# A graph attention kernel on one core: the split of the single-row loads between ScalarE's and SyncE's queues

## The chip, the core and the metric

The kernel runs on one core of a Trainium2 chip. The metric is the device time of one execution in microseconds (us); for a kernel the median over several executions is taken. The core's engines are TensorE (PE in the profile; its weight loads are PEld), VectorE (DVE), ScalarE (ACT), GpSimd (POOL) and SyncE (SP). SyncE computes nothing; it issues DMA transfers. ScalarE computes and issues transfers too: what it issues stands in the profile as ACTq, what SyncE issues as SPq, and an engine handles both kinds of work in the order of its program.

## The reference

One message passing layer over 6250 nodes with 128 features and 206250 edges, sorted by receiver, followed by a residual sum and a layer norm. Cut to what matters:

```python
w_ij  = silu(edge_attr_32 @ rad_W1 + rad_b1) @ rad_W2 + rad_b2
w_ij += silu(edge_attr_32_n2 @ sph_W1 + sph_b1) @ sph_W2 + sph_b2     # (E, 128), 8 heads of 16
alpha = ((x @ Wq)[dst] * w_ij * (x @ Wk)[src]).sum(per head) / 4 * edge_weight
out   = segment_sum(alpha * (x @ Wv)[src], dst) / 16
return layernorm(x + out)
```

The costly access is `[src]`: the senders are in no order, so the key and the value of each edge's sender are fetched from a table row by row.

## The kernel before

**Staging.** A first stage (the first 100 us or so) multiplies all nodes by Wk and Wv and stores one row of 256 floats a node, key and value side by side, in the table `kv_tab` in device memory. The main loop then goes over the edges. A *tile* is 128 edges, a *quad* four tiles (512 edges), a *group* four quads; there are 101 groups and 403 quads. The groups come in order, the quads of a group as 0, 2, 1, 3 (the list `order`). A last stage finishes the last three quads.

**One turn of the main loop** (one quad a turn, number `i`). TensorE sums the messages of the last group (L670), runs the first layers of quad `i+2` (L566), brings the queries to the edges of quad `i+1` (L585) and runs the second layers of `i+1` (L618). The last matmul of L585 gives the one signal of the turn, the *mark*. On it wait: ScalarE's first SiLU of quad `i+2` (L603), VectorE's product of queries and keys of quad `i+1` (L634), GpSimd's next gathers, and SyncE's loads of node rows `x` and edge features. After L634 VectorE goes on with L642, L644, L647 (the scores) and L659 (the messages).

**How the senders' rows arrive.** For most quads GpSimd gathers all four tiles with four indirect DMAs (L142), 14 turns ahead. In 58 quads, spread evenly over turns 8 to 401, the fourth tile is left out of the gathers (L182). Its 128 rows of 1 KB go into a buffer `wide`, each by a DMA of its own (L212) whose address is a number in a register. `ROW_ACT` of these 128 are issued by ScalarE, the rest by SyncE. The addresses are computed and turned in the first stage (`row_bytes`, `turn_rows`) into the table `at_i`, one line for each of the 58 tiles, SyncE's addresses from column `ROW_AT[SP]` and ScalarE's from column `ROW_AT[ACT]`. Register loads (L206) fetch them, up to 32 at a time for SyncE and up to 24 for ScalarE (`ROW_UNITS`).

**What sets the order around the rows.** At the end of each turn `load_rows` hands each engine its share of what is due: the work of a tile (one unit a row, six a register load) is spread evenly over the 6.8 turns (393 / 58) that lie between two such tiles, and it is dealt six turns early (`ROW_LEAD`). SyncE's share goes into its queue among its other transfers, one or two a turn: `x` (L315), `feats` (L252), `relb` (L263), `out` (L777). ScalarE's share stands after its SiLUs; up to two rows of it (`ROW_CARRY`) stand between the two SiLUs of a turn, around a small copy. VectorE waits for the count of all 128 rows (L631) ahead of L634 of that quad, and behind that wait stands all that VectorE does later.

The lines that the change touches are these numbers and the places that read them:

```python
 55 ROW_ACT = 68
 56 ROW_AT = {SP: 0, ACT: 64}
 57 ROW_LOAD = 6
 59 ROW_UNITS = {SP: 32, ACT: 24}
229         n = P - ROW_ACT
230         row_open.append({SP: rows_by(nc.sync, SP, 0, n), ACT: rows_by(nc.scalar, ACT, n, P)})
```

Of the kernel before, what the change touches and what calls it, by code (L numbers as in the profile page):

```python
# [21 lines left out]
SP = mybir.EngineType.SP  # L22
ACT = mybir.EngineType.Activation
# [28 lines left out]
ROW_FIRST = 8  # L52
ROW_LAST = 401
ROW_LEAD = 6
ROW_ACT = 68
ROW_AT = {SP: 0, ACT: 64}
ROW_LOAD = 6
ROW_CARRY = 2
ROW_UNITS = {SP: 32, ACT: 24}
# [14 lines left out]
def gnn_kernel(ctx, tc, x, src, dst, weight, edges, rad_W1, rad_b1, rad_W2, rad_b2,  # L74
# [120 lines left out]
    def open_tile(k):  # L195
# [5 lines left out]
        def rows_by(engine, name, a, b):  # L201
            regs = {}

            def load(e, m):
                c = ROW_AT[name] + e - a
                regs.update(zip(range(e, e + m), nc.values_load_multi_w_load_instructions(  # L206
                    at_i[k:k + 1, c:c + m], engines=(name,), min_val=0,
                    max_val=(N - 1) * ROW_BYTES,
                    skip_runtime_bounds_check_because="senders are nodes")[1]))

            def row(p):
                o = engine.dma_start(row_of[q][p:p + 1, 0, :].bitcast(U8),  # L212
                                     table[:, ds(regs.pop(p), ROW_BYTES)])
                tc.no_tile_sem_insts.add(o.ins.name)
                tc.add_to_no_dep_group(f"rows_{q}", o.ins)
                o.then_inc(row_sems[k % ROW_SEMS], 16)
                row_count[k % ROW_SEMS] += 16
                row_done[q] = row_sems[k % ROW_SEMS], row_count[k % ROW_SEMS]
                row_issued[q] = row_issued.get(q, 0) + 1

            items = []
            for e in range(a, b, ROW_UNITS[name]):
                m = min(ROW_UNITS[name], b - e)
                items.append((ROW_LOAD, lambda e=e, m=m: load(e, m)))
                items += [(1, lambda p=p: row(p)) for p in range(e, e + m)]
            rows_left[name] += items
            return sum(cost for cost, _ in items)

        n = P - ROW_ACT
        row_open.append({SP: rows_by(nc.sync, SP, 0, n), ACT: rows_by(nc.scalar, ACT, n, P)})  # L230
# [108 lines left out]
    with tc.tile_pool(name="nodes", bufs=1) as nodes, \  # L339
# [88 lines left out]
        def turn_rows():  # L428
            pt = nps.tile([P, QT, P], F32, name="pt", bufs=3)
            nc.tensor.transpose(pt[:ROW_TILES, 0, :], rows_f, ident)  # L430
            n = P - ROW_ACT
            for a, b, at in ((0, n, ROW_AT[SP]), (n, P, ROW_AT[ACT])):
                nc.vector.tensor_copy(at_i[:, at:at + b - a], pt[:ROW_TILES, 0, a:b])
# [693 lines left out]
```

## Time and profile before

| what | value |
|---|---|
| median of three runs | 2572.93 us (2570.8 to 2580.83) |
| the profiled execution, and its span | 2581.4 us, 2579.6 us |
| granted TensorE clock, mean | 0.844 of full speed |
| TensorE matmul busy | 2090.3 us, 81% |
| VectorE busy | 1527.9 us, 59% |
| GpSimd busy | 1474.3 us, 57% |
| ScalarE busy | 644.5 us, 25% |
| single-row DMAs issued by ScalarE | 3944 (58 tiles of 68) |
| single-row DMAs issued by SyncE | 3480 (58 tiles of 60) |
| indirect gathers on GpSimd | 1522 |

The page of the profile gives busy time, the chain of work that ended last, and groups of instructions by line. Issuing a DMA is not counted as busy, so ScalarE's 25% leaves out the time in which it issues rows, and SyncE has no busy time at all; how full these two are must be read from the timeline and from the counts of their instructions. A view can be limited to a stretch of the span, and two stretches of one loop can so be compared.

### The profile page before, as it was taken

To read this page: it belongs to the slowest core of one execution; us is meant where nothing else is said; L and a number is where in the kernel's file an instruction comes from. 1 tells how busy PE (TensorE), PEld (TensorE's weight loads), DVE (VectorE), ACT (ScalarE), POOL (GpSimd) and SP (SyncE) were. 2 spreads that over 40 slices of the span, in tenths; PEclk is the share of its full clock that TensorE was granted. 3 is DMA by queue.
4 is the path that set the end of the run, shared out by engine and by line. 5 is a ranking of instruction groups with operands and counts; after the bars stand their busy time and mean duration, and the time that the engine had idled before them with its cause. 6 is when DMAs were issued, how large, how long until landed. Compare 5 with 4: busy or idle time off the path is not lost.

```text
span 2579.6 us, 56198 instructions
## 1 busy us (share of the span) xinstructions
PE 2090.3 (81%) x16002; PEld 1743.4 (68%) x16002; DVE 1527.9 (59%) x3423; ACT 644.5 (25%) x1361; POOL 1474.3 (57%) x1562
## 2 busy tenths in 40 slices
PE   7687888888887878778788788888788888888788
PEld 6566766676666666667667676667566666666677
DVE  5465665656665655555556556556556555566568
ACT  2122222222222222222222222222222222222224
POOL 5565655656565556556566556556565555565550
PEclk8688888878888888888888888878888887888889
DMA  7433434344343434333343433334343443333331
GB/s 272 130 120 105 122 113 124 113 121 122 114 121 114 121 116 122 111 117 113 117 122 114 122 113 121 118 110 124 105 121 114 120 122 110 117 115 121 118 108 38
DMA packets 156799, 307.15 MB, mean 119 GB/s; under 512 B 41798, under 2 KB 90880, under 8 KB 156480
## 3 DMA queue, kind: packets, MB, share of 16 engines
q0 software_dynamic: 74080, 201.69, 27.0%
q1 hardware_dynamic: 72736, 97.22, 11.4%
q10 hardware_dynamic: 9664, 4.58, 0.7%
q8 instruction: 127, 2.08, 0.3%
q14 instruction: 192, 1.57, 0.2%
HBM read 289.88 MB, written 15.11 MB: 118 GB/s over the span
## 4 chain that ended last, share of the span: by engine, by line
PE 33%; issue 20%; DVE 15%; SPq 13%; another core or an unknown queue 12%; ACTq 5%; ACT 1%; DMA 1%; DVEq 0%
PE pw L618 14%; SPq L212 10%; PE pq L585 6%; PE ph L566 5%; ACTq L212 4%; DVE kq L634 3%; DVE side L644 3%; PE po L670 3%; DVE kq L642 3%; SPq L206 2%; PE pk L383 1%; ACTq L206 1%; PE pq L711 1%; DVE side L647 1%
## 5 line engine op out<-in xcount | busy, mean ns | idle before, releaser
L142 POOL DMA_INDIRECT kv<-kv_tab,src_i x1522 | 1442.9, 948 | 1017.6 <-remote 527.7
L618 PE MATMUL pw<-w,act 128*128 128x128 f32 x6448 | 1061.3, 323 | 131.5 <-issue 129.6
L618 PEld LDWEIGHTS pw<-w,act 128*128 128x128 f32 x6448 | 946.4, 229 | 214.3 <-issue 176.5
L603 ACT ACTIVATE act<-ph,b 128x512 f32<-128x512 f32 x806 | 554.6, 689 | 1856.5 <-remote 1559.2
L634 DVE TENSOR_TENSOR kq<-pq,kv 128x512 f32<-128x512 f32 (+1 forms) x404 | 271.1, 671 | 943.8 <-remote 765.7
L566 PE MATMUL ph<-feats,w 32*128 32x512 f32 x1612 | 673.5, 745 | 150.8 <-issue 143.1
L585 PE MATMUL pq<-q,hotT 32*128 32x128 f32 x3224 | 557.1, 321 | 10.0 <-DVE kq L634 6.8
L585 PEld LDWEIGHTS pq<-q,hotT 32*128 32x128 f32 x3224 | 470.8, 220 | 17.0 <-issue 16.7
L566 PEld LDWEIGHTS ph<-feats,w 32*128 32x128 f32 x1612 | 193.2, 209 | 317.4 <-issue 292.0
L644 DVE TENSOR_REDUCE side<-kq 128x32 f32<-128x512 f32 x404 | 280.2, 694 | 14.0
L659 DVE TENSOR_TENSOR msg<-kv,side 128x512 f32<-128x512 f32 (+1 forms) x404 | 269.0, 666 | 13.8
L642 DVE TENSOR_TENSOR kq<-pw,kq 128x512 f32<-128x512 f32 x404 | 274.5, 679 | 0.4 <-PE pw L618 0.4
L670 PE MATMUL po<-msg,hot 128*32 128x128 f32 x3200 | 183.2, 310 | 38.0 <-issue 37.7
L573 PE MATMUL pw<-brow,onesb 3*128 3x512 bf16 x403 | 176.6, 438 | 0.0
L670 PEld LDWEIGHTS po<-msg,hot 128*32 128x32 f32 x3200 | 86.5, 118 | 94.8 <-issue 67.4
L711 PE MATMUL pq<-part,to 128*128 128x128 f32 x196 | 58.4, 389 | 110.3 <-issue 76.1
L711 PEld LDWEIGHTS pq<-part,to 128*128 128x128 f32 x196 | 38.6, 246 | 126.4 <-issue 98.9
L647 DVE TENSOR_TENSOR side<-side,scale 128x32 f32<-128x32 f32 x400 | 79.8, 199 | 13.7
L292 DVE TENSOR_TENSOR hotT<-relb,side 128x512 f32<-128x512 bf16 x101 | 68.7, 680 | 0.0
L297 DVE TENSOR_TENSOR hot<-rel,side 128x512 f32<-128x512 f32 x100 | 68.0, 680 | 0.0
L286 PE MATMUL pq<-wq,xT 128*128 128x128 f32 x200 | 48.8, 331 | 10.0 <-DVE kq L634 7.7
L383 PE MATMUL pk<-wkv,xT 128*128 128x256 f32 x162 | 43.6, 412 | 13.1 <-DVE kv L385 10.0
(132 smaller groups left out, 851.6 us busy)
## 6 DMA issues: line engine op xcount, KB each, us to landing
wide<-kv_tab ACTq DMA_DIRECT2D x3944, 1.0 KB
wide<-kv_tab SPq DMA_DIRECT2D x3480, 1.0 KB
feats<-in_edges SPq DMA_DIRECT2D x101, 512.0 KB
kv<-kv_tab,src_i POOLq DMA_INDIRECT x1522, 2.8
relb<-rel_four SPq DMA_DIRECT2D x101, 128.0 KB
x<-in_x SPq DMA_DIRECT2D x101, 64.0 KB
out<-y SPq DMA_DIRECT2D x101, 64.0 KB
kv_tab<-kv SPq DMA_DIRECT2D x12, 512.0 KB
```

Of the source, the lines that this page charges most:

```text
L142: return nc.gpsimd.indirect_dma_start(out=o, out_offset=None, in_=table, in_offset=bass.IndirectOffsetOnAxis(ap=index, axis=0))
L212: o = engine.dma_start(row_of[q][p:p + 1, 0, :].bitcast(U8), table[:, ds(regs.pop(p), ROW_BYTES)])
L566: return nc.tensor.matmul(act_of[q, i], w1[r0:r0 + R, :], feats_of[g][r0:r0 + R, c0:c0 + EQ], start=True, stop=True)
L573: nc.tensor.matmul(pw, onesb[f:f + 3, :], brow[f:f + 3].rearrange("p t d -> p (t d)"), start=True, stop=False)
L585: o = nc.tensor.matmul(pq_of[q][:, t, :], hotT_of[g][b, t * P:(t + 1) * P], q_of[g][b, :], start=True, stop=True)
L603: o = nc.scalar.activation(act, act_of[q, i], AF.Silu, bias=b1[:, i:i + 1])
L618: o = nc.tensor.matmul(pw[:, t, :], act_of[q, i][:, t * P:(t + 1) * P], w2[:, i, :], start=False, stop=(t == QT - 1 and i == 1))
L634: o = nc.vector.tensor_tensor(kq_of[q][:, u, :], pq_of[q][:, u, :], kv[:, :, :D], op=OP.mult)
L642: nc.vector.tensor_tensor(m, pw_of[q][:, t, :], m, op=OP.mult)
L644: nc.vector.tensor_reduce(alpha, m.rearrange("p t (h e) -> p t h e", e=HD), AX.X, OP.add)
L659: nc.vector.tensor_tensor(msg_of[q][:, u, :].rearrange("p t (h e) -> p t h e", e=HD), kv[:, :, D:].rearrange("p t (h e) -> p t h e", e=HD) ...
L670: o = nc.tensor.matmul(po_of[g][j * W:(j + 1) * W, :], hot_of[g][:, j * QT + t, :], msg_of[g * NQ + j][:, t, :], start=(t == 0), stop=(t = ...
```

## The change

ScalarE issues 72 of the 128 rows of each of the 58 tiles, SyncE 56; before it was 68 and 60. ScalarE's part of the address table starts at column 56 where it started at column 64. The number of register loads stays: SyncE's 56 addresses come in two loads (32 and 24; before 32 and 28), ScalarE's 72 in three (24 each; before 24, 24 and 20).

```diff
-ROW_ACT = 68
-ROW_AT = {SP: 0, ACT: 64}
+ROW_ACT = 72
+ROW_AT = {SP: 0, ACT: 56}
```

On SyncE, in the middle of the main loop, from one load of node rows (`x`) to the next, four turns later. Rows written `wide<-kv_tab` are the single-row DMAs, with their number behind x; `at_i` is the register load of their addresses. Before:

```order
L315 DMA x<-in_x 128x512
L212 DMA wide<-kv_tab 1x1024 x9
L206 TENSOR_LOAD at_i
L777 DMA out<-y_14260 128x512
L212 DMA wide<-kv_tab 1x1024 x7
L263 DMA relb<-rel_four 128x1x512
L212 DMA wide<-kv_tab 1x1024 x10
L252 DMA feats<-in_edges 128x1024
L212 DMA wide<-kv_tab 1x1024 x11
L315 DMA x<-in_x 128x512
```

And now, at the same place:

```order
L315 DMA x<-in_x 128x512
L212 DMA wide<-kv_tab 1x1024 x10
L777 DMA out<-y_14261 128x512
L206 TENSOR_LOAD at_i
L212 DMA wide<-kv_tab 1x1024 x4
L263 DMA relb<-rel_four 128x1x512
L212 DMA wide<-kv_tab 1x1024 x10
L252 DMA feats<-in_edges 128x1024
L212 DMA wide<-kv_tab 1x1024 x10
L315 DMA x<-in_x 128x512
```

In these four turns SyncE has 37 single-row DMAs before and 34 now, and the register load stands behind the store of `out` where it stood ahead of it; the other transfers are the same.

On ScalarE, also in the middle of the main loop: two turns, from the second SiLU of one (`act_104`) to the first SiLU of the turn after the next (`act_99`); `tot` is a small copy. Before:

```order
L603 ACTIVATE act_104<-ph,b_73 128x512
L212 DMA wide<-kv_tab 1x1024 x10
L603 ACTIVATE act_105<-ph,b_73 128x512
L212 DMA wide<-kv_tab 1x1024
L715 ACTIVATE tot<-pq 128x128
L212 DMA wide<-kv_tab 1x1024
L603 ACTIVATE act_106<-ph,b_73 128x512
L212 DMA wide<-kv_tab 1x1024 x10
L603 ACTIVATE act_99<-ph,b_73 128x512
```

And now:

```order
L603 ACTIVATE act_104<-ph,b_73 128x512
L212 DMA wide<-kv_tab 1x1024 x12
L603 ACTIVATE act_105<-ph,b_73 128x512
L212 DMA wide<-kv_tab 1x1024
L715 ACTIVATE tot<-pq 128x128
L212 DMA wide<-kv_tab 1x1024
L603 ACTIVATE act_106<-ph,b_73 128x512
L212 DMA wide<-kv_tab 1x1024 x10
L206 TENSOR_LOAD at_i
L603 ACTIVATE act_99<-ph,b_73 128x512
```

With few exceptions up to 12 rows now stand between the second SiLU of a turn and the first SiLU of the next, where there were up to 11, and the register loads have moved along with the counts. TensorE, VectorE and GpSimd have the same instructions in the same order as before, apart from the widths of the two copies that fill `at_i` (56 and 72 columns).

## The prediction

> **What bounds the kernel now.** I began with the whole page: its first lines and its chain of waits (busy time with share and count; the chain's shares by engine).
>
> ```profile
> span 2579.6 us, 56198 instructions
> PE 2090.3 (81%) x16002; PEld 1743.4 (68%) x16002; DVE 1527.9 (59%) x3423; ACT 644.5 (25%) x1361; POOL 1474.3 (57%) x1562
> PE 33%; issue 20%; DVE 15%; SPq 13%; another core or an unknown queue 12%; ACTq 5%; ACT 1%; DMA 1%; DVEq 0%
> ```
>
> No engine is full, and SyncE, which computes nothing, holds 13% of the chain. So I asked what VectorE waited for (us in total, times, longest), first from 180 to 1014 us, then from 1014 to 2499 us; 1014 is where the first wait of a new kind falls.
>
> ```profile
> DVE kq L634 <- remote: 285.1, 114, 5.7
> DVE kq L634 <- PE pq L585: 26.3, 13, 5.6
> ```
>
> ```profile
> DVE kq L634 <- remote: 441.7, 175, 2.9
> DVE kq L634 <- DVEq L631: 66.4, 16, 9.7
> DVE kq L634 <- PE pq L585: 46.3, 27, 2.9
> DVE kq L634 <- DMA wide<-kv_tab: 20.4, 4, 7.1
> ```
>
> Up to 1014 us VectorE waits only for TensorE's mark. After it, 20 waits with 66.4 + 20.4 = 86.8 us end with the landing of single rows (L631 is the wait for their count). What that costs in pace, the groups by line show for the same two stretches (count, then busy and mean, then idle time before):
>
> ```profile
> L634 DVE TENSOR_TENSOR kq<-pq,kv 128x512 f32<-128x512 f32 (+1 forms) x136 | 91.4, 672 | 312.2 <-remote 285.1 <-PE pq L585 26.3
> L634 DVE TENSOR_TENSOR kq<-pq,kv 128x512 f32<-128x512 f32 (+1 forms) x237 | 159.3, 672 | 580.3 <-remote 441.7 <-DVEq L631 66.4 <-PE pq L585 46.3
> ```
>
> 136 quads in 834 us are 6.132 us each; 237 in 1485 us are 6.266. Which queue is late, the counts of L212's and L206's instructions tell (durations min/median/max in ns, first and last start): from 180 to 1014 us, then L206 in the same stretch, then from 1014 to 2499 us.
>
> ```profile
> L212 ACTq DMA_DIRECT2D wide<-kv_tab x1367: 3/228/772, 180.7 to 1013.9; - x196
> L212 SPq DMA_DIRECT2D wide<-kv_tab x1161: 2/203/1123, 180.3 to 1013.9; - x194
> ```
>
> ```profile
> L206 SPq TENSOR_LOAD <-at_i x39: 938/1917/2249, 193.5 to 1013.9; - x39
> ```
>
> ```profile
> L212 SPq DMA_DIRECT2D wide<-kv_tab x2101: 2/204/1462, 1015.4 to 2498.9; - x191
> ```
>
> The program deals SyncE 58 x 60 / 393 = 8.855 rows a turn. 136 turns ask for 1204; it issued 1161, so it fell back by 43, and 43/60 of a tile at 834 / (1161/60) = 43.1 us a tile is a head start of 31 us used up. Over the next 237 turns 2099 are asked for and 2101 issued: VectorE goes at SyncE's pace. ScalarE owes 58 x 68 / 393 = 10.04 a turn, 1365 for 136 turns, and issued 1367: it keeps up. That SyncE is full, and not held up, its own waits from 180 to 2499 us show; the first and last of the five that are listed:
>
> ```profile
> SPq L315 <- DVE y L732: 0.7, 1, 0.7
> ...
> SPq L252 <- remote: 0.2, 1, 0.2
> ```
>
> None is over 0.7 us. So there are two regimes: up to 1014 us the gathers and TensorE set 6.132 us a quad; after it SyncE's queue sets 6.266.
>
> **The change part by part.** It moves 4 rows a tile, 232 in all. *SyncE.* Its timeline in the middle of the loop (start, us, what, count):
>
> ```profile
> 1010.12 0.74 SPq L777 DMA_DIRECT2D out<-y  x1
> 1010.89 5.08 SPq L212 DMA_DIRECT2D wide<-kv_tab  x5
> 1016.02 0.56 SPq L263 DMA_DIRECT2D relb<-rel_four  x1
> 1016.68 6.17 SPq L212 DMA_DIRECT2D wide<-kv_tab  x11
> ```
>
> One of the other transfers takes 0.7 us to the next start, and there is one a turn. In the first stretch rows got 834 - 39 x 1.92 (loads) - 136 x 0.7 = 664 us, or 0.572 us a row; the eleven here agree (6.17 / 11 = 0.56). Four rows fewer save 2.29 us a tile: 43.1 becomes 40.8, against 6.776 turns x 6.132 = 41.55 that a tile lasts at the first regime's pace. SyncE then has 0.75 us a tile to spare and never loses its 31 us. The low bound for a row is 0.31 us, its price where no gathers run (rows below): then a tile takes 41.85 us and SyncE loses 0.3 us a tile, 17 us over 58 tiles, still within the 31. So the gain does not hang on this price. If the second regime goes, its 237 quads take 237 x 6.132 = 1453 us in place of 1485: **32 us less**. The other readings bracket it: idle time ahead of L634 rose from 312.2/136 = 2.30 to 580.3/237 = 2.45 us, 36 us over 237 quads; the waits themselves are 86.8 us, of which 20 x 2.30 = 46 would have been spent on the mark, leaving 41. I take 31.
>
> *ScalarE.* It gets 0.59 rows more a turn. Its timeline (idle before a SiLU in brackets):
>
> ```profile
> 1026.70 0.69 ACT L603 ACTIVATE act<-ph,b 128x512 f32<-128x512 f32 x1 [4.84 <-remote]
> ...
> 1027.47 4.69 ACTq L212 DMA_DIRECT2D wide<-kv_tab  x11
> 1033.02 0.69 ACT L603 ACTIVATE act<-ph,b 128x512 f32<-128x512 f32 x1 [4.88 <-remote]
> ...
> 1040.38 5.41 ACTq L212 DMA_DIRECT2D wide<-kv_tab  x11
> 1045.84 0.69 ACT L603 ACTIVATE act<-ph,b 128x512 f32<-128x512 f32 x1 [4.85 <-remote]
> ```
>
> Eleven rows end at 1032.16, 0.86 us ahead of the next SiLU, or at 1045.79, with nothing to spare: 0.43 to 0.49 us a row here, 0.31 at best. A twelfth row hides in the first case and makes the SiLU late by up to 0.5 us in the second. Does that lateness reach the next mark? At the end of the loop GpSimd has no gathers left and the same turn runs with ScalarE and SyncE issuing at once:
>
> ```profile
> 2518.89 0.69 ACT L603 ACTIVATE act<-ph,b 128x512 f32<-128x512 f32 x1 [2.84 <-DVEq L631]
> ...
> 2519.66 3.40 ACTq L212 DMA_DIRECT2D wide<-kv_tab  x11
> 2519.85 3.12 SPq L212 DMA_DIRECT2D wide<-kv_tab  x10
> 2523.12 0.69 ACT L603 ACTIVATE act<-ph,b 128x512 f32<-128x512 f32 x1 [2.79 <-issue]
> ```
>
> That turn lasts 4.2 us from first SiLU to first SiLU, and ScalarE's issue ends it. So the loop through ScalarE and TensorE closes in about 4.2 us, and a SiLU late by 0.5 us has some 2 us of cover in a 6.2 us turn. The cover is the gathers:
>
> ```profile
> 1020.66 0.95 POOL L142 DMA_INDIRECT kv<-kv_tab,src_i  x1 [1.53 <-remote]
> ...
> 1024.42 0.95 POOL L142 DMA_INDIRECT kv<-kv_tab,src_i  x1 [0.30 <-issue]
> 1026.93 0.95 POOL L142 DMA_INDIRECT kv<-kv_tab,src_i  x1 [1.56 <-remote]
> ```
>
> Four of them, 1.25 us apart, then the mark: 6.27 us from set to set. I charge 2 us for lateness that gets through (none to 20: of the 16 turns from 1000 to 1095 us the timeline shows five that leave under 0.4 us, so some 120 of 390 turns would be late by 0.17 us on average). In the last eleven turns the cover is gone and every row counts: 11 x 0.59 x 0.31 = **2 us more**. Register loads cost nothing new, since their number stays and only their length changes.
>
> *The sum:* 2581.4 - 31 + 2 + 2 = 2554 for the profiled execution. That one lies 8.5 us over the median of 2572.93. Whether its excess sits in the row waits no view shows: if it does, the median gains 27 - 8.5 = 18.5, if not 27. I take 25, so **2548 us**; its own range is 2538 to 2560.
>
> **The rivals.** *One generator for both queues.* If the rows of the two queues went through one unit, SyncE's 0.57 us would be its wait for ScalarE's rows, and four rows moved would come back as four waits: no gain, 2573. For it speaks that a row on SyncE costs 0.57 us beside ScalarE's 0.31 to 0.49. Against it speak the rows at 2519: ten on SyncE and eleven on ScalarE in the same 3.4 us, each at 0.31. Chance 0.13. [...]
>
> *The throttle takes it back.* With VectorE's stalls gone TensorE gets less rest, and its granted clock could fall (columns: stretch, its length, VectorE's work on `wide`, clock, DMA share, GB/s):
>
> ```profile
> 180.00:1014.00 834.00, 11.21 (x40) 0.85 0.40 118
> 1014.00:2499.00 1485.00, 19.64 (x70) 0.84 0.39 117
> ```
>
> The denser stretch had 0.85, the other 0.84, which speaks against it. If it took half: 2573 - 13 = 2560. Chance 0.10.
>
> *ScalarE becomes the pace (slower).* If a late first SiLU delays its mark one for one, each added row is on the path: 232 x 0.31 to 0.49 = 72 to 114 us at most. It outweighs the 31 us once more than about a third of the rows (31 / (232 x 0.4) = 0.33) get through; with 60% it is 232 x 0.4 x 0.6 = 56, less 31, so about 2598. For it speak the turn at 1045 and the end of the loop; against it the 2 us of cover. Chance 0.12.
>
> *The change doesn't do what it says:* the order shows 56 and 72 rows and unchanged loads; 0.01, no time of its own.
>
> **How the numbers follow.** Forecast 0.64, shared generator 0.13, throttle 0.10, ScalarE 0.12. A change of 0.5%, 13 us, is what a measurement here can tell from none, so faster means below 2560 and slower above 2586. The forecast and half of the throttle's case are faster: 0.69. The shared generator and the other half are the same: 0.18. ScalarE's case and the remainder are slower: 0.13. The range runs from 2533 (the 41 us reading, with no loss) to 2578, which takes in no gain at all with the runs' scatter, and leaves out the slower case.
>
> **What the profile after would show.** Waits of L634 on L631 and on `wide` gone or below 10 us, 237 quads of the second stretch at about 6.13 us, and SyncE waiting now and then for marks ahead of `x` and `feats`. ScalarE's SiLUs would start right behind its rows more often, without longer turns. I am wrong if row waits stay (generator), if L634 waits as long as before but for the mark (ScalarE or the throttle, told apart by the granted clock), or if the last turns grow by more than a few us.

## The result and the profile after

| | before | after |
|---|---|---|
| median of four runs, us | 2576.88 (2570.8 to 2582.33) | 2551.26 (2549.95 to 2553.56) |
| the profiled execution and its span, us | 2581.4, 2579.6 | 2552.35, 2550.6 |
| granted clock | 0.844 | 0.842 |

The ratio is 0.9896, with a 95% interval from 0.9872 to 0.9920: 26 us less, where 25 were forecast. The median of before has a fourth run in it here; with three it was 2572.93, from which the prediction reckoned, and so 3 us lie between the forecast of 2548 and the median after.

The page of the changed kernel: first its span, then the chain's shares by engine.

```profile
span 2550.6 us, 56198 instructions
PE 46%; DVE 19%; another core or an unknown queue 15%; issue 15%; ACTq 4%; ACT 1%; DVEq 0%; DMA 0%; SPq 0%
```

SyncE's share of the chain went from 13% to 0%, and TensorE's from 33% to 46%. The chain follows one path back and jumps at close calls, so the waits decide. What VectorE waited for, from 180 to 1014 us and, in the second fence, from 1014 to 2478 us, where the loop now ends:

```profile
DVE kq L634 <- remote: 291.4, 117, 5.3
DVE kq L634 <- PE pq L585: 19.3, 13, 2.8
```

```profile
DVE kq L634 <- remote: 507.5, 205, 3.1
DVE kq L634 <- PE pq L585: 46.8, 24, 3.2
DVE kq L634 <- issue: 0.4, 1, 0.4
```

The 66.4 us on L631 and the 20.4 us on `wide` are gone; VectorE waits for the mark alone in both stretches. (`remote` is the profile's word for a wait whose signal it can't match with work that has just ended. Of the 335 such waits of L634 in the whole profile, 334 end within 0.06 us of an update of the semaphore that carries TensorE's mark; the update itself comes some 3 us after the modelled end of the matmul, on which see the last section.) The groups of L634 in the same two stretches:

```profile
L634 DVE TENSOR_TENSOR kq<-pq,kv 128x512 f32<-128x512 f32 (+1 forms) x136 | 91.4, 672 | 311.1 <-remote 291.4 <-PE pq L585 19.3
L634 DVE TENSOR_TENSOR kq<-pq,kv 128x512 f32<-128x512 f32 (+1 forms) x239 | 160.5, 672 | 555.6 <-remote 507.5 <-PE pq L585 46.8 <-issue 0.4
```

The first stretch holds 136 quads as before, so nothing changed while SyncE was still ahead. The second holds 239 in 1464 us, 6.126 us a quad where it was 6.266: both stretches now go at one pace. SyncE's rows in both stretches, and the longest of its own waits from 180 to 2478 us:

```profile
L212 SPq DMA_DIRECT2D wide<-kv_tab x1119: 3/197/882, 182.5 to 1013.8; - x187
```

```profile
L212 SPq DMA_DIRECT2D wide<-kv_tab x1973: 2/198/1477, 1014.5 to 2477.6; - x198
```

```profile
SPq L315 <- remote: 10.0, 11, 2.4
SPq L252 <- remote: 7.2, 16, 1.7
SPq L252 <- PE pq L585: 6.8, 5, 2.4
```

The program deals 58 x 56 / 393 = 8.265 rows a turn: 1124 for 136 turns, 1975 for 239. SyncE issued 1119 and 1973, so it falls back by 7 rows in both stretches together, some 5 us of its head start, where before it lost 43 rows in the first stretch alone. Now and then it stands still ahead of `x` and `feats` until TensorE's mark lets it go on; all its waits come to 26 us. Before, its longest wait there was 0.7 us. The clock is the same as before in both stretches (length, VectorE's work on L634, clock, DMA share, GB/s):

```profile
180.00:1014.00 834.00, 95.34 (x156) 0.85 0.40 119
1014.00:2478.00 1464.00, 167.60 (x275) 0.84 0.40 119
```

### The profile page after: what moved, and what is told of

Its sections match the earlier page's. It is cut to its first block, busy times and chain, and to the rows that moved or that the text cites. A ratio compares the mean times of both kernels' runs of the same rounds, so it can differ in the third digit from the quotient of the medians.

```text
span 2550.6 us, 56198 instructions
## 1 busy us (share of the span) xinstructions
PE 2090.7 (82%) x16002; PEld 1750.2 (69%) x16002; DVE 1528.3 (60%) x3423; ACT 643.0 (25%) x1361; POOL 1474.5 (58%) x1562
## 4 chain that ended last, share of the span: by engine, by line
PE 46%; DVE 19%; another core or an unknown queue 15%; issue 15%; ACTq 4%; ACT 1%; DVEq 0%; DMA 0%; SPq 0%
PE pw L618 21%; PE pq L585 8%; PE ph L566 8%; DVE kq L634 4%; DVE side L644 4%; PE po L670 4%; DVE kq L642 3%; ACTq L212 3%; PE pq L711 1%; PE pk L383 1%; DVE side L647 1%; DVE hotT L292 1%; PE pq L713 1%; DVE hot L297 1%
## 5 line engine op out<-in xcount | busy, mean ns | idle before, releaser
L618 PEld LDWEIGHTS pw<-w,act 128*128 128x128 f32 x6448 | 957.9, 232 | 192.4 <-issue 155.8
L603 ACT ACTIVATE act<-ph,b 128x512 f32<-128x512 f32 x806 | 554.6, 689 | 1827.6 <-remote 1627.4
L634 DVE TENSOR_TENSOR kq<-pq,kv 128x512 f32<-128x512 f32 (+1 forms) x404 | 271.1, 671 | 913.5 <-remote 834.0
L585 PE MATMUL pq<-q,hotT 32*128 32x128 f32 x3224 | 556.4, 321 | 2.2 <-issue 2.1
L585 PEld LDWEIGHTS pq<-q,hotT 32*128 32x128 f32 x3224 | 469.6, 220 | 3.3 <-issue 3.2
L647 DVE TENSOR_TENSOR side<-side,scale 128x32 f32<-128x32 f32 x400 | 79.8, 199 | 13.7
```

What stands on the lines that cost most here:

```text
L585: o = nc.tensor.matmul(pq_of[q][:, t, :], hotT_of[g][b, t * P:(t + 1) * P], q_of[g][b, :], start=True, stop=True)
L603: o = nc.scalar.activation(act, act_of[q, i], AF.Silu, bias=b1[:, i:i + 1])
L618: o = nc.tensor.matmul(pw[:, t, :], act_of[q, i][:, t * P:(t + 1) * P], w2[:, i, :], start=False, stop=(t == QT - 1 and i == 1))
L634: o = nc.vector.tensor_tensor(kq_of[q][:, u, :], pq_of[q][:, u, :], kv[:, :, :D], op=OP.mult)
```

## The experiments

The experiments ran on four chips, on each with the kernel before beside them. The chips were of two kinds. On two of them the kernel before took 2562 to 2583 us, as in the result; on the other two 1963 to 1971 us. Each experiment below names its kind as the *slow chip* or the *quick chip*; a ratio always compares runs on one chip.

**1. SyncE alone relieved, ScalarE alone relieved.** Five single rows of a tile become one DMA of five neighbouring table rows, on one engine, with everything else as before:

```diff
+            def five(p):
+                at = regs.pop(p)
...
+                o = engine.dma_start(row_of[q][p:p + 5, 0, :].bitcast(U8),
+                                     flat[ds(at, 5 * ROW_BYTES)].rearrange("(p b) -> p b", p=5))
...
-                items += [(1, lambda p=p: row(p)) for p in range(e, e + m)]
+                first = e + 5 if name == SP and e == a else e
+                if first > e:
+                    items.append((1, lambda p=e: five(p)))
+                items += [(1, lambda p=p: row(p)) for p in range(first, e + m)]
```

> The kernel before (68 and 60), but SyncE fetches the first five of its rows of a tile with one DMA of five neighbouring table rows: 56 DMAs a tile on SyncE, ScalarE's 68 stay. It leaves four of the 128 right senders out of each of the 58 tiles. Theory (SyncE's queue is the bound, what ScalarE takes over is hidden): as the changed kernel or up to 4 us less, 2547 to 2551 us, no waits of VectorE on rows. Shared generator: 124 DMAs a tile through one unit in place of 128, so it gains as well, about 2551. If instead the gain came from how ScalarE's part was laid out anew (its loads and rows at other places), it stays at 2573 to 2577.

> The kernel before, but ScalarE fetches the first five of its rows of a tile with one DMA of five neighbouring table rows: 64 DMAs a tile on ScalarE, SyncE's 60 stay. It leaves four of the 128 right senders out of each of the 58 tiles. Theory (SyncE's queue is the bound): no gain, 2570 to 2580 us, about 87 us of waits of VectorE on rows as before, SyncE still at 43 us a tile in its free run. Shared generator: SyncE waits for four rows fewer, so 2551. ScalarE as the bound: faster as well.

These fell on a quick chip: 1968.03 and 1963.24 us beside 1964.78, ratios 1.0006 (0.9986 to 1.0025) and 0.9989 (0.9970 to 1.0008). Neither moves anything: there SyncE's queue is no bound, as the last section shows. The same pair on another chip:

> The kernel with 56 DMAs a tile on SyncE (five rows in one) and ScalarE's 68 kept, again, for a chip on which the kernel before takes about 2575. Theory (SyncE's queue is the bound there): as the changed kernel or up to 4 us less, 2543 to 2551, no waits of VectorE on rows. If the gain came from ScalarE's new layout: 2575. On a chip on which the kernel before takes 1965: no change, as measured.

> The kernel with 64 DMAs a tile on ScalarE (five rows in one) and SyncE's 60 kept, again. Theory (SyncE's queue is the bound where the kernel before takes about 2575): no gain, 2567 to 2582, the waits of VectorE on rows stay near 87 us. Shared generator: about 2550, as SyncE would wait for four rows fewer. On a chip on which the kernel before takes 1965: no change, as measured.

On a slow chip: 2536.21 and 2564.49 us beside 2570.31. With SyncE relieved the ratio is 0.9862 (0.9834 to 0.9890), 34 us; with ScalarE relieved by as many DMAs 0.9979 (0.9964 to 0.9995), 6 us. VectorE's waits from 1014 to 2440 us, with SyncE relieved, then with ScalarE relieved (the added lines shift the numbers: L650 is the old L634, L647 the old L631):

```profile
DVE kq L650 <- remote: 487.0, 197, 3.2
DVE kq L650 <- PE pq L601: 45.4, 25, 3.4
```

```profile
DVE kq L650 <- remote: 438.7, 177, 3.4
DVE kq L650 <- DVEq L647: 52.9, 13, 7.0
...
DVE kq L650 <- DMA wide<-kv_tab: 9.4, 2, 5.3
```

The row waits vanish in the first and remain, somewhat shorter, in the second. So the gain comes from SyncE's side, and not from the new layout of ScalarE's rows. A generator that both queues share one for one is out, since relieving ScalarE would then have given about 2550 us, and it gave 2564. Where the 6 us come from is not shown; a weak coupling of the two queues is one possible cause.

**2. The same step the other way.**

```diff
-ROW_ACT = 68
+ROW_ACT = 64
```

> The other way: ScalarE 64, SyncE 64. Theory (0.572 us a row on SyncE): a tile takes SyncE 43.1 + 4 x 0.572 = 45.4 us against 41.55 that the loop needs, the head start of 31 us is used up after 8 tiles, and the other 50 lose 3.1 to 3.9 us each (SyncE ran 1.7% faster while VectorE waited): 2551 + 153 to 190 = 2704 to 2741 us. With 0.31 us a row: a tile of 44.35, 47 tiles at 2.8, less 1.7%: 2648 to 2683. Shared generator: no change, 2573.

On the quick chip nothing: 1967.04 us, ratio 1.0005 (0.9981 to 1.0028).

> ScalarE 64, SyncE 64, again. Theory with 0.572 us a row on SyncE (where the kernel before takes about 2575): 2700 to 2741; with 0.31 us a row 2648 to 2683; shared generator 2575. On a chip on which the kernel before takes 1965: no change, as measured.

On the slow chip, the one of the pair above: 2642.10 us, ratio 1.0279 (1.0252 to 1.0306), 72 us more. The direction is as expected, the size is not: it lies below both ranges. The first wait on rows falls at 516 us, with the ninth such tile, so the head start lasted the 8 tiles that were expected; with 60 DMAs (ScalarE relieved) it falls at 1217 us, with the 26th. L634 in the 1426 us from 1014 to 2440 us gives SyncE's pace, in turn with 64 DMAs a tile, with 60 (ScalarE relieved) and with 56 (SyncE relieved, where the gathers set the pace):

```profile
L634 DVE TENSOR_TENSOR kq<-pq,kv 128x512 f32<-128x512 f32 (+1 forms) x222 | 149.1, 672 | 581.1 <-remote 365.7 <-DVEq L631 99.5 <-PE pq L585 47.4
```

```profile
L650 DVE TENSOR_TENSOR kq<-pq,kv 128x512 f32<-128x512 f32 (+1 forms) x230 | 154.5, 672 | 550.5 <-remote 438.7 <-DVEq L647 52.9 <-PE pq L601 34.4
```

```profile
L650 DVE TENSOR_TENSOR kq<-pq,kv 128x512 f32<-128x512 f32 (+1 forms) x233 | 156.6, 672 | 533.6 <-remote 487.0 <-PE pq L601 45.4 <-issue 0.4
```

A tile is 6.776 turns: 43.5, 42.0 and 41.5 us. Four rows from 60 to 64 cost 1.5 us a tile, so one more row costs SyncE about 0.38 us and not 0.572. In the run with 60 the first 200 us of this window still go at the gathers' pace; from the 25th such tile to the 56th, a tile takes 42.1 us with 60 and 43.5 with 64, which makes 0.36. With 0.38 the head start of 31 us lasts 31 / (43.1 + 1.5 - 41.5) = 10 tiles, and the other 48 lose 43.5 - 41.5 = 2.0 us each, where 3.1 to 3.9 were expected: 2536 + 96 = 2632, 10 us from what was measured. As the 43.5 us are taken from the same run, this shows that head start and pace together account for the time; it is no forecast.

**3. The changed kernel again.**

> The changed kernel itself once more (72 and 56). In the four runs before this one the kernel before took 1965 us in place of 2577, and neither fewer rows on SyncE nor more changed it. If the kernel before takes about 2577 here: 2551, as measured, by the theory that SyncE's queue is the bound there. If it takes about 1965: SyncE is no bound, so no gain; ScalarE's four rows more a tile then lie beside a turn of 4.8 us, and by the run with one copy more (109 us of ScalarE's time made it 266 us longer) ScalarE is the pace, so 232 rows of 0.31 to 0.43 us, 72 to 100 us, come on top of 1965: 2037 to 2065; if they are hidden, 1965.

On the other slow chip: 2547.25 us beside 2572.34, ratio 0.9904 (0.9884 to 0.9924), the first result once more.

> The changed kernel, beside the next three on one chip. Where the kernel before takes about 2572: 2547 (0.990 of it). Where it takes 1965: hidden, 1965, or 2037 to 2065 if ScalarE is the pace there.

On a quick chip: 1964.92 us beside 1966.01, ratio 0.9997 (0.9983 to 1.0011). The change gains nothing there and costs nothing.

**4. How much more ScalarE can take.** These ran on the quick chips alone, so the questions that they were to settle for the slow ones stay open.

> Five rows in one DMA on both engines: 56 DMAs a tile on SyncE and 64 on ScalarE; it leaves eight of the 128 right senders out of each of the 58 tiles. Beside 56 and 68 (0.986 of the kernel before) and 56 and 72 (0.990) it gives the price of ScalarE's rows with SyncE out of the way. Theory (nearly all of ScalarE's issue is covered by the gathers): 0 to 5 us below 56 and 68, that is 0.984 to 0.986 of the kernel before; if four rows on ScalarE cost the 10 us that lie between the two runs so far: 0.982.

1963.77 us, ratio 0.9991 (0.9977 to 1.0005): nothing.

```diff
-ROW_ACT = 72
+ROW_ACT = 76
```

> ScalarE 76, SyncE 52, with a fourth register load on ScalarE a tile (24, 24, 24, 4). SyncE has nothing more to give. Theory: a little over the changed kernel, since 4 rows and a load, some 3.3 us of ScalarE's time a tile, make more first SiLUs late, of which little gets through: 2550 to 2560 where the kernel before takes 2572. ScalarE as the pace: 58 x 3.3 = 191 us, a third of it 64: over 2600.

2024.85 us, ratio 1.0299 (1.0282 to 1.0317), 59 us more. Its chain of waits, by line:

```profile
ACTq L212 52%; ACTq L206 13%; ACT act L603 5%; PE pw L618 3%; PE ph L566 2%; PE pq L585 1%; PE pk L383 1%; DMA msg<-in_x,src_x 1%; DVE kq L634 1%; ACT y L746 1%; DVE side L644 0%; DVE kq L642 0%; PE po L670 0%; ACT q L288 0%; POOL msg L142 0%
```

ScalarE's rows and register loads now hold 65% of the chain; in the changed kernel on the same chip they hold 32%. So on a quick chip the split of 72 and 56 is hidden, and the next step, four rows and a fourth register load, is not.

```diff
+    scratch = const.tile([P, 128], F32, name="scratch")
...
+            nc.scalar.activation(scratch, act[:, :128], AF.Copy)
```

> The changed kernel (72 and 56) with one more copy of 128x128 on ScalarE after each second SiLU, 0.27 us a turn, 109 us in all, into a scratch tile that nobody reads. Theory (a late first SiLU is covered by the gathers, GpSimd's four and the wait behind them set 6.13 us a turn): 3 us from the last eleven turns and a few more, 2553 to 2561. ScalarE as the pace: a third or more of the 109 us gets through, 2587 to 2660.

> The changed kernel with one more 128x128 copy a turn on ScalarE (0.27 us, 109 us in all, read by nobody). Where the kernel before takes 2572: by the theory of the cover 2550 to 2565; ScalarE as the pace: 2587 or more. Where it takes 1965: about 2231, as measured.

2230.97 us beside 1964.78 and 2229.63 beside 1966.01, ratios 1.1344 (1.1325 to 1.1363) and 1.1344 (1.1328 to 1.1360). The copies took 0.31 us each, 125 us in all and not 109, and made the kernel 264 to 266 us longer. The timeline of ScalarE shows a cause, first without the copy (the changed kernel on a quick chip), then with it (L604 is L603, L213 is L212, L613 the copy):

```profile
1000.38 0.69 ACT L603 ACTIVATE act<-ph,b 128x512 f32<-128x512 f32 x1 [2.23 <-PE pq L585]
...
1001.12 0.69 ACT L603 ACTIVATE act<-ph,b 128x512 f32<-128x512 f32 x1
1001.14 3.47 ACTq L212 DMA_DIRECT2D wide<-kv_tab  x11
```

```profile
1002.41 0.69 ACT L604 ACTIVATE act<-ph,b 128x512 f32<-128x512 f32 x1
1003.13 0.31 ACT L613 ACTIVATE scratch<-act 128x128 f32<-128x128 f32 x1
1003.20 0.23 ACTq L213 DMA_DIRECT2D wide<-kv_tab  x1
```

Without the copy the rows begin 0.02 us behind the start of the second SiLU and are issued while it computes. The copy starts only when that SiLU has ended, and all rows behind it wait with it: they begin 0.79 us behind the SiLU's start. Over all turns with such rows the medians are 0.05 and 0.79 us. That is the price a turn, not 0.27: 403 x 0.74 = 298 us, of which 265 got through. The granted clock also fell, from 0.95 to 0.90; whether that added to the 265 is not shown. As a dose of ScalarE time the copy was mis-sized, and this run says nothing about four rows more.

## Why the prediction was right

**The bound.** Two regimes, the second set by SyncE's queue: shown, for the slow chips. Relieving SyncE alone removes the row waits and 34 us; relieving ScalarE alone leaves the waits and gains 6; loading SyncE with four rows more costs 72.

**The gain of 31 us.** The second stretch went from 6.266 to 6.126 us a quad, where 6.132 was forecast: 237 x 0.140 = 33 us in that profile. The forecast that 237 quads would take the first stretch's pace is the step that carried the number, and it held. From profiled execution to profiled execution the sum said 27 us less, and it was 2581.4 - 2552.35 = 29. For the median the prediction chose 25 between 18.5 and 27, so that it lies within 1 us of the measured 26 is partly luck.

**SyncE's price of a row.** 0.572 us was too high for a row that is added: 0.36 to 0.38 is what it measured between 60 and 64. The likely reason is that the mean over a stretch holds delays that do not come with the number of rows; no run tried this by itself. For rows taken away the price was not measured. With 0.572 SyncE would have 0.75 us a tile to spare; its waits in the profile after, 26 us over some 55 tiles, are 0.5 us a tile. The forecast did not hang on the price, since even 0.31 kept SyncE's loss within its head start. The expectation for 64 rows did hang on it, and missed.

**The register loads.** The prediction counted them as free, since only their length changes. The profiles show that the length counts: from 180 to 2478 us a load of 20 addresses on ScalarE took 1.55 us before (medians), one of 24 took 1.79 before and after; on SyncE 28 addresses took 1.89 us before and 24 take 1.33 after. That is some 0.24 us a tile more on ScalarE, 14 us over 58 tiles, and some 0.56 us a tile less on SyncE. How much of it reached the time is not shown. The 0.36 to 0.38 us a row from 60 to 64 hold a load of four addresses more.

**ScalarE's 2 us for lateness.** In the profile before, set against the updates of the mark's semaphore, a first SiLU starts more than 0.1 us late at 7 of the 320 turns of the main loop (turns 10 to 386) that have four gathers; after, at 27, where the prediction's upper bound was made of some 120. After, those 27 last at the median 6.37 us from mark to mark, the other turns 6.32; before, 6.31 and 6.32. So 27 x 0.05 = 1.4 us more, about the size of the charge, but it rests on differences far smaller than the scatter of single turns, and it was read from two profiles and not tried by itself. Between 56 and 68 with a ratio of 0.9862 and 56 and 72 with 0.9896 and 0.9904 lie some 10 us, but on different chips and with intervals that overlap; whether four rows on ScalarE cost 2 or 10 us on a slow chip stays open.

**The last eleven turns, 2 us.** Not seen. From the product of the quad of the 56th such tile to the end it was 2579.6 - 2499.1 = 80.5 us and is 2550.6 - 2471.0 = 79.6.

**The rivals.** The throttle took nothing back: the clock is 0.85 and 0.84 in the two stretches, as before; that less rest lowers it, no run here shows. ScalarE is not the pace on the slow chips at 72 rows (ACTq has 4% of the chain); on the quick chips it is at 76 (65% of the chain, 59 us more). A generator shared one for one would have let both reliefs gain alike, and they gained 34 and 6 us, so it is out; a weaker coupling of the two queues could explain the 6 us that relieving ScalarE gained (1 to 9 by its interval), but not the 34.

## What to carry to other kernels

A queue without busy time can be the bound: compare, stretch by stretch, what the program deals it with what it issued, and look whether it ever waits. A head start hides such a bound in the first part of a loop, so two stretches of one loop say more than its mean (here 6.132 and 6.266 us a quad), and the stretch in which the queue was still ahead gives the time without the bound. What one more instruction costs on a queue need not be the mean over its instructions: one more row here cost 0.36 to 0.38 us, where the mean was 0.572. An instruction that must wait for the engine can delay everything issued behind it by the whole wait: a copy of 0.31 us behind a SiLU put the rows behind it 0.74 us later. A bound that is found on one chip need not be the bound on another: the same change gave a ratio of 0.9896 on a slow chip and of 0.9997 on a quick one.

## What was not expected of the hardware

The same program took 2551 us on one chip and 1965 on another. Both profiles of the changed kernel have GpSimd's gathers at the same 0.95 us and 1.25 us apart. What differs is when the mark arrives, and how fast SyncE issues. On a slow chip, the end of the matmuls of L585, the turn's last gather and the next first SiLU:

```profile
1030.08 0.60 PE L585 MATMUL pq<-q,hotT 32*128 32x128 f32 x4
...
1031.74 0.95 POOL L142 DMA_INDIRECT kv<-kv_tab,src_i  x1 [0.30 <-issue]
1034.27 0.69 ACT L603 ACTIVATE act<-ph,b 128x512 f32<-128x512 f32 x1 [5.10 <-remote]
```

And on a quick one:

```profile
1005.06 0.60 PE L585 MATMUL pq<-q,hotT 32*128 32x128 f32 x4
...
1005.76 0.69 ACT L603 ACTIVATE act<-ph,b 128x512 f32<-128x512 f32 x1 [3.95 <-PE pq L585]
```

3.6 us lie between the matmul's modelled end and the SiLU on the one, 0.1 us on the other; on the slow chip the SiLU starts 1.6 us after the end of GpSimd's last gather of the turn. Over whole profiles, the mark's semaphore is updated 2.8 to 3.0 us (medians) after the modelled end of its matmul in all six profiles on the slow chips, and 0.05 to 0.06 us in all eight on the quick ones. The single rows differ too, though the kernel is the same. On the quick chip, from 180 to 1014 us:

```profile
L212 SPq DMA_DIRECT2D wide<-kv_tab x1500: 227/228/504, 180.0 to 1013.4; - x188
```

No row's issue there is shorter than 227 ns, and SyncE issued 1500 rows in the time in which it got 1119 done on the slow chip, with 112 us of waits against 15. From one row to the next SyncE takes 0.66 to 0.73 us (medians) in the profiles on the slow chips and 0.32 in those on the quick ones. On the slow chip both delays end with the gathers: in the profile before, the last one ends at 2508.9 us; the next twelve marks are updated 0.05 to 0.09 us after the matmul, and SyncE takes 0.32 us from row to row, where from 180 to 2478 us it was 3.05 and 0.71 us (medians). So what runs beside the gathers is delayed on the one kind of chip and hardly on the other, TensorE's signal and SyncE's issue alike.

What bounds the changed kernel on the quick chip is GpSimd. Its largest kind of wait, in the changed kernel on a slow chip and then on a quick one:

```profile
POOL kv L142 <- remote: 556.7, 344, 3.3
```

```profile
POOL kv L142 <- issue: 402.5, 1319, 0.3
```

On the slow chip GpSimd waits for marks; on the quick one none of these waits is longer than 0.3 us, and of the 1521 steps from one gather to the next 1517 are shorter than 1.35 us. 1522 gathers of 1.25 us are 1903 of the 1963 us. With 64 rows on each queue, or with five rows in one DMA, it is the same on the quick chips (1516 to 1519 steps). VectorE waits there too on L631, which also stands for the count of the gathers:

```profile
DVE kq L634 <- DVEq L631: 173.2, 120, 3.1
```

Of these 120 waits 114, with 168 us, are at quads without single rows, so they are for gathers; in the slow profile before, all waits on L631 and on `wide` are at quads with single rows. That is why on the quick chips neither four rows more on SyncE nor four rows fewer change the time. The granted clock differs too, 0.84 against 0.95 on the mean, but the late mark does not come from the lower clock: in the profile after on the slow chip, from 180 to 2478 us, the update came 3.3 us after the matmul (median of 276 marks) where the granted clock was full and 2.6 us (99 marks) where it was half. How much of the 586 us between the chips is the clock's is not shown. Nor does any run here show what makes the chips differ; as each chip was measured on one occasion only, chip and occasion can't be told apart.
